# Layer 1 of a four-layer graph network: the W1v g products of two blocks as four 64x64 products on the quarters of TensorE

## The chip, the cores and the metric

The kernel runs on one core of one Trainium2 chip. The metric is the device time of one execution in microseconds (us). TensorE, VectorE, ScalarE and GpSimd are called PE, DVE, ACT and POOL in the profile; PEld is the loading of weights into TensorE, which overlaps its products.

## What is computed

Four graph layers, each a residual with a layer norm ahead of it, work on x of shape (8, 2048, 64) with one normalised adjacency matrix adj of 2048 x 2048. The change is in layer 1, which takes three steps:

```python
def _L1_gnn_ref(causal_vars, adj_matrix, intervention_value, W1, b1, W2, b2, intervention_idx):
    v = causal_vars.at[:, intervention_idx].set(intervention_value)
    for _ in range(MAX_STEPS):                                   # 3
        effects = jnp.einsum('nm,bmd->bnd', adj_matrix, v)
        h = jnp.concatenate([v, effects], axis=-1)
        h = jax.nn.relu(jnp.einsum('bnk,dk->bnd', h, W1) + b1)   # W1 is 64 x 128
        v = jnp.einsum('bnk,dk->bnd', h, W2) + b2
    return v
...
h = jnp.maximum(_layernorm(x, axis=-1), 0.0)
x = x + _L1_gnn_ref(h, adj, ...)
```

W1 falls into a half for v (W1v) and a half for the neighbours' sum (W1e). So each step needs W1v v, and adj times W1e v.

## The kernel before

**Two batches share the 128 partitions.** A tile in feature layout is 128 x 512: partitions 0 to 63 hold the 64 features of one batch, 64 to 127 those of the next, and the 512 columns are nodes. The 8 batches are NP = 4 pairs p, and the 2048 nodes are NB = 4 blocks nb. The weights are laid out to match, as 128 x 128 matrices with the 64 x 64 weight twice on the diagonal and zeros elsewhere (`make_weights`, L620 to L633). All of layer 1 stays in the form g, the value after the relu: from the second step on W2 is multiplied into the weights, so that W1v v is `w1v2` times g (in the first step `w1vT` times v), with the biases folded in.

**One block of one step** (`layer1`, L869 to L925) is made of these parts:

- `product` (L243 to L254): adj times the node-layout tiles u for the block's 512 nodes. For each of 16 chunks m it issues two matmuls (H and L, the high and low parts of u in a reduced fp32 format, L250, output `bv`), 32 in all. Its argument `fill` names work that is put into TensorE's program behind chunk m. Then `scaled` (L240, on VectorE) multiplies by the row `crow` into the tile g.
- `ph` (L897, L900 to L902): W1v times the block's old g, called gT here. It is an fp32 product of the full array, 128 x 128 weights and 512 columns, put behind m = 12, into a PSUM bank of the tag "tr".
- L904, on VectorE: g = ph + g. L905, on ScalarE: g = relu(g + bias).
- `finish` (L876 to L886) turns a finished g back to nodes with four small products (`back_to_nodes`, L661 to L666, in PSUM tiles of the tag "big"), and in the first two steps splits the result into H and L for the next step (`halves`, L230 on ScalarE and L232 on VectorE). It stands behind the product of the next block, so that the relu has time; that of the third block is put behind m = 8 of the fourth.

Around these, VectorE tests in the first two steps that the adjacency has the expected form (L846), and the last step prepares the next pair p (`prepare_next`, L672 to L684: transposes into gT by `to_feat`, L267 the copy) and the norm ahead of layer 2.

**PSUM** has eight banks: the tags "mm" (product), "tr" (transposes, ph) and "big" (two banks to a tile), two buffers each. **The order** of each engine's work is the program's, except where a planner moves an instruction behind others because it reckons that its operands come later, and where `tc.issue_after` ties one instruction behind another.

**Layer 0 has the only products of this kernel that divide the array.** `node_weights` (L697 to L728) works on 64 of the 128 partitions at a time (`bb` = 0 and 1, output `y`, L711), each with 64 x 128 weights and 512 columns, into a PSUM bank of its own. They are used below as a yardstick.

Of the kernel before, what the change touches and what calls it, by code (L numbers as in the profile page):

```python
# [8 lines left out]
F32 = mybir.dt.float32  # L9
# [5 lines left out]
ALU = mybir.AluOpType  # L15
# [27 lines left out]
def uniform_path(  # L43
# [30 lines left out]
    nc = tc.nc  # L74
    P = 128
    B, N, C = x.shape
# [9 lines left out]
    psums = [pro.enter_context(tc.tile_pool(name="psump", bufs=1, space=bass.MemoryType.PSUM))]  # L86
# [14 lines left out]
    def bank(tag, name):  # L101
        return psums[-1].tile([P, 512], F32, tag=tag, name=name)
# [31 lines left out]
    def nodes(acc):  # L134

        return acc.rearrange("p j f -> p (j f)").rearrange("p (e j c) -> p j e c", e=2, c=C)

    def load_x(layer, p, nb, queue=nc.sync):
        acc = block("acc", f"acc_{layer}_{p}_{nb}", 2)
        fill_x(acc, layer, p, nb, queue)  # L140
        return acc
# [11 lines left out]
    def load_crow(nb, name, tag="crow"):  # L153
        t = work.tile([P, 512], F32, tag=tag, name=f"crow_{name}", bufs=2)
        nc.sync.dma_start(t, crowD[:, nb * 512:(nb + 1) * 512].to_broadcast([P, 512]))
        return t
# [4 lines left out]
    def split(t):  # L161
        return t.rearrange("p j (b c) -> p j b c", b=2)
# [45 lines left out]
    def go_on():  # L208

        with tc.issue_after(ahead.pop().ins) if ahead else nullcontext():  # L210
            for e in list(pending):
                next(e[0])
                e[1] -= 1
                if e[1] == 0:
                    pending.remove(e)
        ahead.clear()
# [8 lines left out]
    def halves(src, name, pool=None, later=None):  # L225

        pool, bufs = (work, 6) if pool is None else (pool, 4)
        Hq = pool.tile([P, 4, 2 * C], F32R, tag="H", name=f"H_{name}", bufs=bufs)
        Lq = pool.tile([P, 4, 2 * C], F32R, tag="L", name=f"L_{name}", bufs=bufs)
        copies.append(nc.scalar.copy(Hq, src))  # L230
        def rest():
            lows.append(nc.vector.tensor_tensor(Lq, src, Hq.bitcast(F32), op=ALU.subtract))  # L232

        rest() if later is None else later.append(rest)
        return Hq, Lq
# [9 lines left out]
    def product(hl, nb, name, out, crow, fill={}, tag="mm"):  # L245

        ps = bank(tag, f"bv_{name}")
        for m in range(NCH):
            for i in range(2):
                nc.tensor.matmul(  # L250
                    ps, hl[m // 4][i][:, m % 4, :], BT[:, m, nb * 512:(nb + 1) * 512],
                    start=(m == 0 and i == 0), stop=(m == NCH - 1 and i == 1),
                )
            if m in fill:  # L254
                fill[m]()
        return scaled(ps, out, crow)
# [308 lines left out]
    nm = "0_1_3a"  # L565
    tx = work.tile([P, 512], F32, tag="z", name=f"t1T_{nm}", bufs=3)
    ps = bank("b1", f"bv_{nm}")
    for m in range(NCH):
        if m in (2, 7, 12):
            go_back(1 + m // 5)  # L570
        for i in range(2):
            nc.tensor.matmul(
                ps, hls[1][m // 4][i][:, m % 4, :], BT[:, m, 3 * 512:],
                start=(m == 0 and i == 0), stop=(m == NCH - 1 and i == 1),
# [80 lines left out]
    def feat(i, name):  # L655

        if i == 0:
            return term(1, name)
        return lastp[0].tile([P, 512], F32, tag="fm", name=name, bufs=4)

    def back_to_nodes(fT, wmat, name, tag="big"):  # L661

        ps = psums[-1].tile([P, 4, 2 * C], F32, tag=tag, name=f"bn_{name}")
        for t in range(4):
            nc.tensor.matmul(ps[:, t, :], fT[:, t * P:(t + 1) * P], wmat, start=True, stop=True)  # L665
        return ps  # L666
# [5 lines left out]
    def prepare_next(n, q):  # L672
        if n >= len(items):
            return
        layer, p = items[n]
        nm = f"{layer}_{p}_{q}"
        hl, gT = ops.setdefault(n, ([], []))
        h = load_h(p, q, nm, lastp[0] if n else l0q)
        if layer == 1:
            if q == 0:  # L680
                nc.scalar.copy(h[0:1, 0, :], ivt)
            gT.append(to_feat(h, feat(0, f"gT_{nm}"), nm))
            h = back_to_nodes(gT[q], w1e, f"u_{nm}", "big" if n else "mm")
        hl.append(halves(h, nm))  # L684

    def rows4(r):
        return r.rearrange("p (b c) -> p b c", b=2)[:, None].to_broadcast([P, 4, 2, C])

    def keep(p, nb, acc, name, more):

        norm_relu(acc, name, lambda z: nc.gpsimd.dma_start(hs[p][:, part(nb), :], z))  # L691
        nc.gpsimd.tensor_tensor(nodes(acc), nodes(acc), more, op=ALU.add)  # L692
        kept.append(nc.gpsimd.dma_start(xs[p][:, part(nb), :], acc))
# [36 lines left out]
    def feat_0(p, q):  # L730
        h = load_h(p, q, f"f0_{p}_{q}", l0q)
        return to_feat(h, term(0, f"t0T_{p}_{q}"), f"0_{p}_{q}")

    first_t0 = []
    for p in range(NP):
# [47 lines left out]
        for nb in range(NB):  # L783
            nm = f"0_{p}_{nb}b"
# [3 lines left out]
                fill={12: lambda: first_t0.append(feat_0(0, 0))} if p + nb == 0 else {},  # L788
                tag="mm" if p + nb else "b0",
# [32 lines left out]
    w1vT, w1eT, w2T, wos, w1v2, w1e2, r1e, rbo = (wl[:, i, :] for i in range(8))  # L822
# [18 lines left out]
    def test(k):  # L841

        i, q = divmod(k, NB)
        st, mt = tested[k]
        junk = lastp[0].tile([P, 512], U8, name="junk")
        nc.vector.scalar_tensor_tensor(  # L846
            junk, mt, cols[:, i, :], st, op0=ALU.mult, op1=ALU.not_equal,
            accum_out=bad[:, i, q:q + 1],
        )
        test_load()  # L850
# [18 lines left out]
    def layer1(n, p):  # L869
        hl, gT = ops[n]  # L870
        steps = 3
        for s in range(steps):
            last = s == steps - 1
            g_new, hl_new = [], []

            def finish(nb):  # L876
                nm = f"1_{p}_{s}_{nb}"
                if last:
                    acc = load_x(1, p, nb)
                    pn = back_to_nodes(g_new[nb], w2T, nm)  # L880
                    nc.vector.tensor_tensor(nodes(acc), split(pn), nodes(acc), op=ALU.add)
                    keep(p, nb, acc, f"2_{p}_{nb}", rows4(rbo))
                else:
                    pn = back_to_nodes(g_new[nb], w1e2, nm)
                    nc.vector.tensor_tensor(split(pn), split(pn), rows4(r1e), op=ALU.add)
                    hl_new.append(halves(pn, nm))  # L886

            def mid():
                if last:
                    prepare_next(n + 1, 2)  # L890
                else:
                    finish(2)

            for nb in range(NB):
                nm = f"1_{p}_{s}_{nb}"
                crow = load_crow(nb, nm)
                ph = bank("tr", f"ph_{nm}")  # L897
                g = feat((s + 1) % 2, f"g_{nm}")
                fill = {8: mid} if nb == 3 else {}
                fill[12] = lambda: nc.tensor.matmul(  # L900
                    ph, w1v2 if s else w1vT, gT[nb], start=True, stop=True
                )  # L902
                product(hl, nb, nm, g, crow, fill=fill)
                gadd = nc.vector.tensor_tensor(g, ph, g, op=ALU.add)  # L904
                nc.scalar.activation(g, g, AF.Relu, bias=b1s if s else b1c)  # L905
                g_new.append(g)
                go_on()
                if nb in (1, 2):
                    finish(nb - 1)
                    if last:  # L910
                        prepare_next(n + 1, nb - 1)
                if s < 2:
                    k = 2 * (8 * p + 4 * s + nb)
                    with tc.issue_after(gadd.ins):
                        test(k)
                        test(k + 1)
            if last:
                finish(2)
                prepare_next(n + 1, 3)
            if last and n == NP - 1:  # L920

                put_off.append(lambda: finish(3))
            else:
                finish(3)
            gT, hl = g_new, hl_new  # L925
# [81 lines left out]
    for n, (layer, p) in enumerate(items):  # L1007
        (layer1, layer2)[layer - 1](n, p)
        if n == NP - 1:
            test_end()  # L1010
# [593 lines left out]
```

## Time and profile before

The median of three runs is 1248.38 us (1244.74 to 1248.88). The profiled run has a span of 1245.5 us.

| | |
|---|---|
| TensorE busy | 1211.7 us of the span |
| VectorE / ScalarE / GpSimd busy | 745.5 / 181.7 / 223.9 us |
| layer 1, about | 632 to 1085 us |
| the largest two groups of bv (L250), H and L | 426.3 and 401.0 us busy, 1024 matmuls each |
| ph (L900) | 48 products, 96 matmuls |
| granted TensorE clock | 0.994 |

In the page's groups a product in full fp32 shows up as two matmuls with the same names, and two weight loads. A matmul's end is modelled and its start is recorded, so what a matmul takes of TensorE is read from the distance of starts. The chain that ended last is followed back from the last instruction of the kernel, each time to what released it; the share of an engine in it is the share of the span in which that engine's work, and not a wait for another, held up the end.

### The profile page before, as it was taken

What the parts mean: (1) busy time and instruction counts of PE and PEld (TensorE: products, weight loads), DVE (VectorE), ACT (ScalarE), POOL (GpSimd) and SP (SyncE); (2) the same over time, 40 slices, a digit from 0 to 9 for tenths busy, and PEclk for the clock granted to TensorE, in tenths of its full rate; (3) what the DMA queues carried; (4) which work ended last, traced back from release to release, by engine and by line L of the source; (5) the groups of instructions that cost most, each with busy time, mean ns of one, the idle gap of its engine ahead of it and who ended that gap; (6) DMA issues with size and microseconds to landing.
All of it is one profiled execution on the core that took longest, in us unless ns stands there. A gap on an engine that the chain in (4) does not pass through costs nothing.

```text
span 1245.5 us, 15336 instructions
## 1 busy us (share of the span) xinstructions
PE 1211.7 (97%) x5702; PEld 860.6 (69%) x5702; DVE 745.5 (60%) x1940; ACT 181.7 (15%) x281; POOL 223.9 (18%) x233
## 2 busy tenths in 40 slices
PE   5999999999999999999999999999999999999995
PEld 4775555555665557655577888788788878888884
DVE  5356888777757774477654445445543545566664
ACT  6610001000010000000111121112111211211100
POOL 5410222211131111011110022003101300231211
PEclk9999999999999999999999999999999999999998
DMA  9951334332332232122265436533643553433311
GB/s 358 372 142 53 101 107 115 85 87 72 90 106 67 65 89 79 51 64 64 60 148 135 110 100 153 116 90 119 161 106 90 152 127 96 128 137 117 115 56 46
DMA packets 100984, 140.98 MB, mean 113 GB/s; under 512 B 43772, under 2 KB 58108, under 8 KB 98852
## 3 DMA queue, kind: packets, MB, share of 16 engines
q1 hardware_dynamic: 82820, 80.74, 24.8%
q0 software_dynamic: 11776, 48.15, 13.0%
q10 hardware_dynamic: 6304, 11.01, 2.7%
q8 instruction: 47, 0.77, 0.2%
q14 instruction: 37, 0.30, 0.1%
HBM read 95.03 MB, written 35.66 MB: 105 GB/s over the span
## 4 chain that ended last, share of the span: by engine, by line
PE 93%; DMA 3%; DVE 3%; POOL 1%; issue 0%; ACT 0%; SPq 0%; POOLq 0%; ACTq 0%
PE bv L250 38%; PE y L711 26%; PE bn L665 5%; PE ph L900 3%; PE bv_2b L250 2%; PE bv_1b L250 2%; PE bv_3b L250 2%; PE bv_0b L250 2%; DMA BT<-in_adj_dram 2%; PE bn_u L665 1%; PE bv_0a L250 1%; PE bv_3a L250 1%; PE pt L262 1%; PE bv_2a L250 1%; PE pS L949 1%; PE bv_1a L250 1%
## 5 line engine op out<-in xcount | busy, mean ns | idle before, releaser
L250 PE MATMUL bv<-BT,H 128*128 128x512 f32 x1024 | 426.3, 416 | 0.0
L250 PE MATMUL bv<-BT,L 128*128 128x512 f32 x1024 | 401.0, 392 | 0.0
L250 PEld LDWEIGHTS bv<-BT,H 128*128 128x128 f32 x1024 | 192.5, 188 | 47.8 <-issue 11.6
L250 PEld LDWEIGHTS bv<-BT,L 128*128 128x128 f32 x1024 | 192.7, 188 | 47.5 <-issue 11.5
L720 DVE SCALAR_TENSOR_TENSOR acc<-y,emb,acc 128x128 f32<-128x128 f32 x512 | 176.2, 344 | 65.7 <-PE y L711 65.7
L720 DVE SCALAR_TENSOR_TENSOR odd<-y,emb,odd 128x128 f32<-128x128 f32 x448 | 153.3, 342 | 0.0
L711 PE MATMUL y<-wt,t0T 64*128 64x512 f32 x512 | 143.7, 607 | 2.4 <-DVE odd L720 1.7
L240 DVE TENSOR_TENSOR g<-bv,crow 128x512 f32<-128x512 f32 x48 | 33.2, 692 | 183.2 <-PE bv L250 183.2
L194 POOL TENSOR_TENSOR rstd<-var,mhalf 128x8 f32<-128x8 f32 x64 | 105.7, 1653 | 180.6 <-DVE var L191 174.8
L186 ACT ACTIVATE sq<-z 128x512 f32<-128x512 f32 x64 | 40.4, 631 | 406.6 <-DVE z L181 396.6
L711 PEld LDWEIGHTS y<-wt,t0T 64*128 64x128 f32 x512 | 45.8, 185 | 63.3 <-issue 57.1
L692 POOL TENSOR_TENSOR acc<-acc,b2r 128x512 f32<-128x512 f32 x16 | 22.2, 1389 | 315.5 <-DVE z L181 315.5
L692 POOL TENSOR_TENSOR acc<-acc,wl 128x512 f32<-128x512 f32 x16 | 20.7, 1291 | 299.3 <-DVE z L181 299.2
L711 PE MATMUL y<-wt,t1T 64*128 64x512 f32 x256 | 66.8, 589 | 0.0
L197 DVE SCALAR_TENSOR_TENSOR z<-z,rstd 128x512 f32<-128x512 f32 x64 | 44.7, 703 | 35.5 <-POOL rstd L194 35.5
L665 PEld LDWEIGHTS bn<-wl,g 128*128 128x128 f32 x384 | 49.5, 191 | 5.1 <-ACT g L905 1.5
L189 DVE TENSOR_REDUCE var<-sq 128x8 f32<-128x512 f32 x64 | 43.6, 681 | 15.6 <-ACT sq L186 15.6
L665 PE MATMUL bn<-wl,g 128*128 128x128 f32 x384 | 51.1, 276 | 0.0
L846 DVE SCALAR_TENSOR_TENSOR junk<-mt,cols,st 128x512 uint8<-128x512 bf16 x64 | 47.7, 745 | 4.1 <-DMA mt<-MD 3.7
L711 PEld LDWEIGHTS y<-wt,t1T 64*128 64x128 f32 x256 | 27.1, 187 | 27.8 <-issue 27.8
L905 ACT ACTIVATE g<-g,b1s 128x512 f32<-128x512 f32 x32 | 23.2, 724 | 137.2 <-DVE g L904 137.1
L691 POOL DMA_DIRECT2D hs<-z x32 | 18.6, 582 | 133.6 <-DVE z L197 97.0
(210 smaller groups left out, 1672.4 us busy)
## 6 DMA issues: line engine op xcount, KB each, us to landing
BT<-in_adj_dram POOLq DMA_DIRECT2D x16, 1024.0 KB, 19.5
crow<-crowD SPq DMA_DIRECT2D x64, 256.0 KB, 3.3
st<-in_adj_dram SPq DMA_DIRECT2D x64, 256.0 KB, 3.6
hs<-z POOLq DMA_DIRECT2D x40, 256.0 KB, 3.2
xs<-acc POOLq DMA_DIRECT2D x32, 256.0 KB, 2.4
MD<-BT POOLq DMA_DIRECT2D x16, 512.0 KB, 5.6
acc<-xs SPq DMA_DIRECT2D x32, 256.0 KB, 3.9
hb<-hs SPq DMA_DIRECT2D x28, 256.0 KB, 3.3
```

The costliest lines, as they stand in the source:

```text
L186: squares.append(nc.scalar.activation(sq, z, AF.Square))
L189: nc.vector.tensor_reduce(var, groups(sq), axis=AX.X, op=ALU.add)
L194: powers.append(nc.gpsimd.tensor_tensor(rstd, var, mhalf, op=ALU.pow))
L197: scales.append(nc.vector.scalar_tensor_tensor(groups(h), g, 0.0, rstd[:, :, None].to_broadcast([P, 8, C]), op0=ALU.max, op1=ALU.mult))
L240: ahead.append(nc.vector.tensor_tensor(to, ps.rearrange("p (q t) -> p t q", t=4), crow, op=ALU.mult))
L250: nc.tensor.matmul(ps, hl[m // 4][i][:, m % 4, :], BT[:, m, nb * 512:(nb + 1) * 512], start=(m == 0 and i == 0), stop=(m == NCH - 1 and i ...
L665: nc.tensor.matmul(ps[:, t, :], fT[:, t * P:(t + 1) * P], wmat, start=True, stop=True)
L692: nc.gpsimd.tensor_tensor(nodes(acc), nodes(acc), more, op=ALU.add)
L711: nc.tensor.matmul(y[:, bb, :], terms[k][hs_, ts], wt[hs_, k, dg * 512:(dg + 1) * 512], start=(k == 0), stop=(k == K - 1),)
L720: last = nc.vector.scalar_tensor_tensor(xj, yd, ec, old, op0=ALU.mult, op1=ALU.add)
L846: nc.vector.scalar_tensor_tensor(junk, mt, cols[:, i, :], st, op0=ALU.mult, op1=ALU.not_equal, accum_out=bad[:, i, q:q + 1],)
L900: fill[12] = lambda: nc.tensor.matmul(ph, w1v2 if s else w1vT, gT[nb], start=True, stop=True)
```

## The change

The product of the full array multiplies two 64 x 64 blocks of zeros along with the two that count. The change takes two blocks nb and nb + 1 together and gives each quarter of the array one product of its own: the two batches (bb) of two blocks (i). Weights of batch bb are on its partitions, and the output of the second block comes out on the partitions of the other batch (`two[bb ^ i]`), so that the four products lie on four different quarters. They write two PSUM banks, one for each half of the rows, in a tile of the tag "big". ScalarE then copies each quarter to where its old g was (gT, in place), on the partitions of its batch, and L904 adds that tile instead of the PSUM bank. The four products stand behind m = 10 of the even blocks; the odd blocks have none. The aim is that the four products take the time of one.

```diff
+            def map_two(nb):
+
+                ph = psums[-1].tile([P, 2, 512], F32, tag="big", name=f"ph_1_{p}_{s}_{nb}")
+                w = w1v2 if s else w1vT
+                two = (slice(0, C), slice(C, P))
+                for i in range(2):
+                    for bb in range(2):
+                        nc.tensor.matmul(
+                            ph[two[bb ^ i], bb, :], w[two[bb], two[bb]], gT[nb + i][two[bb], :],
+                            start=True, stop=True,
+                        )
+                for i in range(2):
+                    for bb in range(2):
+                        nc.scalar.copy(gT[nb + i][two[bb], :], ph[two[bb ^ i], bb, :])
+
             for nb in range(NB):
                 nm = f"1_{p}_{s}_{nb}"
                 crow = load_crow(nb, nm)
-                ph = bank("tr", f"ph_{nm}")
                 g = feat((s + 1) % 2, f"g_{nm}")
                 fill = {8: mid} if nb == 3 else {}
-                fill[12] = lambda: nc.tensor.matmul(
-                    ph, w1v2 if s else w1vT, gT[nb], start=True, stop=True
-                )
+                if nb % 2 == 0:
+                    fill[10] = lambda: map_two(nb)
                 product(hl, nb, nm, g, crow, fill=fill)
-                gadd = nc.vector.tensor_tensor(g, ph, g, op=ALU.add)
+                gadd = nc.vector.tensor_tensor(g, g, gT[nb], op=ALU.add)
                 nc.scalar.activation(g, g, AF.Relu, bias=b1s if s else b1c)
```

## The prediction

> **What bounds the kernel now.** I read the page from the top (busy shares, then the chain of work that ended last), then the groups and busy times of the stretch in which layer 1 runs, then single instructions around one of the products that the change touches.
>
> ```profile
> PE 1211.7 (97%) x5702; PEld 860.6 (69%) x5702; DVE 745.5 (60%) x1940; ACT 181.7 (15%) x281; POOL 223.9 (18%) x233
> PE 93%; DMA 3%; DVE 3%; POOL 1%; issue 0%; ACT 0%; SPq 0%; POOLq 0%; ACTq 0%
> PE bv L250 38%; PE y L711 26%; PE bn L665 5%; PE ph L900 3%; PE bv_2b L250 2%; PE bv_1b L250 2%; PE bv_3b L250 2%; PE bv_0b L250 2%; DMA BT<-in_adj_dram 2%; PE bn_u L665 1%; PE bv_0a L250 1%; PE bv_3a L250 1%; PE pt L262 1%; PE bv_2a L250 1%; PE pS L949 1%; PE bv_1a L250 1%
> ```
>
> TensorE is 93% of the chain, and the products that change (ph, L900) are 3% of it. The table by stretches says how tight layer 1 is (columns: length, then busy time and instructions of PE, weight loads, VectorE, ScalarE, GpSimd):
>
> ```profile
> 632.00:1085.00 453.00, 453.00 (x2159) 363.73 (x2159) 217.13 (x418) 78.54 (x128) 59.48 (x59) 1.00 0.50 122
> L904 DVE TENSOR_TENSOR g<-ph,g 128x512 f32<-128x512 f32 x48 | 33.0, 688 | 1.1
> L267 ACT COPY gT<-pt 128x512 f32<-128x512 f32 x12 | 7.0, 586 | 60.1 <-PE pt L262 60.1
> PEld bn L665 <- ACT g L905: 1.5, 8, 0.2
> ```
>
> TensorE has no gap in 453 us, at full clock; VectorE is busy 48% of it and ScalarE 17%. TensorE waits for a relu (L905) for 1.5 us in all. So in this stretch a microsecond of TensorE taken away or added is a microsecond of the span, and the other engines have room.
>
> What one ph costs is read from starts, since ends are modelled (columns: start, length, engine):
>
> ```profile
> 689.90 0.39 PE L250 MATMUL bv<-BT,L 128*128 128x512 f32 x1
> 690.13 1.02 PE L900 MATMUL ph<-g,wl 128*128 128x512 f32 x2
> 690.58 0.80 PE L250 MATMUL bv<-BT,H 128*128 128x512 f32 x1
> 691.22 0.40 PE L250 MATMUL bv<-BT,L 128*128 128x512 f32 x1
> ```
>
> From one bv to the bv after next, without a ph, it is 2 x 0.227 = 0.454 us (starts 689.90 and 690.13 are 0.23 apart). Here it is 691.22 - 689.90 = 1.32. So one ph, an fp32 product written as two matmuls of 0.43 us each, costs 0.867 us; taken over all 48 of them the median is 0.868. In all 48 x 0.868 = 41.7 us, the 3% of the chain.
>
> The trace has no 64x64 quarter. It has the nearest thing, the y products of layer 0 (L711): 64 rows x 128 columns, bb = 0 on the upper and bb = 1 on the lower half of the rows, each two matmuls again:
>
> ```profile
> 401.14 1.05 PE L711 MATMUL y<-wt,t1T_1a 64*128 64x512 f32 x4
> 402.00 1.05 PE L711 MATMUL y<-wt,t2T_1b 64*128 64x512 f32 x4
> 401.14 0.22 PEld L711 LDWEIGHTS y<-wt,t1T_1a 64*128 64x128 f32 x2 [0.21 <-issue]
> ```
>
> Four matmuls, which are two whole products, take 0.86 us: the two halves of the rows run side by side. More than that: the four fill 1.05 = 0.43 + 0.59 + 0.03, so they start in two pairs, 0.03 apart within a pair (two loads of 0.187 fill 0.22). Had the second product waited for the second matmul of the first, as program order has it, four would fill three steps, 1.45. So a product on other rows overtakes the second half of the one before it.
>
> Those groups also show what it costs to change the division of the array:
>
> ```profile
> 412.44 1.05 PE L711 MATMUL y<-wt,t2T_1b 64*128 64x512 f32 x4
> 413.42 0.50 PE L250 MATMUL bv_2b<-BT,H_t 128*128 128x512 f32 x1
> 413.75 0.39 PE L250 MATMUL bv_2b<-BT,L_t 128*128 128x512 f32 x1
> ...
> 420.81 0.60 PE L262 MATMUL pt<-ident,hb_f 128*128 128x128 f32 x4
> 421.34 1.13 PE L711 MATMUL y<-wt,t0T 64*128 64x512 f32 x4
> 422.30 1.02 PE L711 MATMUL y<-wt,t1T_2a 64*128 64x512 f32 x4
> ```
>
> Out: the y group would be done at 412.44 + 0.86 = 413.30, and the second bv would start at 413.53; it starts at 413.75, 0.22 late (0.21 to 0.24 over 15 such places). In: the four transposes end their turn at 420.81 + 4 x 0.107 = 421.24; the second k would start at 422.10 and does at 422.30, 0.20 late (0.20 in nearly all). A round trip costs 0.43 us.
>
> **What the Trainium skill says.** "TensorEngine Tiling (Array Packing)", Key Properties: tiles work independently, and a change of tiling mode drains TensorE. The trace agrees for row tiles, with 0.43 us for a round trip. "TensorE: Matmul & The Clock Gate", Part 3, has single-pass products on tiles divided both ways running together, 16 of them 10.6 times as fast; it also says that matmuls start in strict program order. The first half isn't shown here for column tiles; the second disagrees with the y group above, and the trace decides. "FP8 and Floating Point Precision", TensorE Precision Notes: true fp32 takes four passes; the two matmuls of 0.43 us per ph fit that. "PSUM — Partial Sum Buffer", on bank collisions: different row tiles must not write one bank together. The change gives each half of the rows its own bank, so nothing has to be serialised for that.
>
> **The change part by part.** Per pair of blocks (24 pairs: 4 p x 3 s x 2):
> - *Removed:* two ph, 2 x 0.868 = 1.736 us of TensorE, on the path.
> - *Added on TensorE:* one round trip, 0.435 by the y groups (bounds 0.3 to 0.7, as the columns are divided too), and four products as eight matmuls. If all four quarters run together, as the two row halves do, that is 2 x 0.43 + about 0.06 of starts one after another (the pairs above were 0.03 apart) = 0.92. If only the rows overlap, it is twice that of a y pair: 1.72. If a row half takes its matmuls strictly in order but lets the two column halves overlap, there are three steps: 1.29. I take 0.92: the overtaking seen in y says that a matmul waits for its own tile and not for the stream, and the four tiles share neither rows with columns nor banks across rows.
> - *Sum for the likeliest case:* 1.736 - 0.92 - 0.435 = 0.38 us per pair, x 24 = 9.1 us.
> - *ScalarE:* four copies of 64x512, priced at the 0.586 us of the 128x512 copy from PSUM (fewer partitions, same elements in each): 2.34 us per pair, 56 us over layer 1, so ScalarE goes from 17% to 30% busy. Nothing of it is on the path: the map stands after m = 10, so 10 bv (2.27 us) of the product follow. The copies for the even block are done some 1.2 to 1.4 us after the map, 1 us before the block's bv end; L904 comes 0.9 us after the end (bv end 692.38, L904 at 693.30). The other two copies end about 0.2 us after it, still before L904, and the block they are for comes a product (9 us) later. Behind the copies on ScalarE stand the relu L905, 1.6 us after the product's end, and the H copies of a block finished at the start of the product, done long before.
> - *VectorE:* L904 reads two SBUF tiles in place of PSUM and SBUF; a sum of two SBUF tiles (L727) takes 679 ns, L904 688. It now waits for ScalarE instead of TensorE; behind it is the test L846, with no hurry. Cost nothing.
> - *PSUM:* two banks of the tag "big" for about 3.5 us per pair, next to the back_to_nodes tiles (L663). There are two buffers, and those tiles come every few microseconds; the next one after a map takes the other buffer. In the last step, where two come together, the second needs the map's: it follows transposes and a copy, by then the map is copied. Nothing, at most 0.5 us in 4 places.
> - *Order:* nothing is waited for earlier than before, except that gT of the second block is read one product sooner; it is a step old.
>
> **The rivals.**
> - *Three steps* (a row half is in order): 24 x (1.736 - 1.29 - 0.435) = 0.3 us less, 1248. For it: the overtaking is shown between rows only. Against: I know of no reason why columns should differ.
> - *Columns don't overlap*: 24 x (1.72 + 0.435 - 1.736) = 10 us more, 1258.4, slower. For it: both column halves of a row half are fed from the same 64 partitions, and no column tile is in the trace. Against: the skill's 16 tiles.
> - *The copies become a wait*: were relu, and with it a back_to_nodes, 0.5 us late in the 8 places that have no slack (the 1.5 us row) the gain would shrink by 4 us, to 1243.
>
> **How the numbers follow.** Before: 1248.38, with 1244.74 lowest. Quarters together: 0.57, 1248.4 - 9.1 = 1239.3. Three steps: 0.20, 1248. Columns in turn: 0.18, 1258. Late copies: 0.05, 1243. The range runs from 1235.5 (a cheap round trip of 0.3, 12.4 us saved) to 1251 (three steps with a dearer round trip), which leaves out columns in turn and a little at the ends. Faster by over 3.7 us: the first case less a tenth for a dear round trip, and half of the fourth, 0.55. Within: 0.23. Slower: 0.22.
>
> **What would show it.** Right: from the last bv before the map to the second bv after it about 0.45 + 1.35 us; eight ph matmuls in two clumps 0.43 apart; layer 1 some 9 us shorter with TensorE still without a gap; ScalarE near 135 us in it. Three clumps and 0.45 + 1.73 is the first rival, four clumps the second. Idle time of bn L665 before ScalarE's g beyond 1.5 us would be the third. The prediction is wrong if entering or leaving quarters costs far more than 0.43 us, or a column half has to wait for the other.

## The result and the profile after

The changed kernel takes 1239.24 us (median of 4, 1238.1 to 1241.54) where the kernel before takes 1247.76 (median of 4, 1244.74 to 1248.88): a ratio of 0.9938, with a 95% interval of 0.9915 to 0.9961. Run once more beside the experiments it gave 1237.89 us and 0.9923 (0.9908 to 0.9937). So it is 8 to 10 us faster, and the 1239.3 of the prediction was met. How it was met is another matter: two terms were off, in opposite directions, and they nearly cancel.

The page after, first the busy time by engine, then the chain that ended last:

```profile
PE 1197.7 (97%) x5798; PEld 843.7 (68%) x5798; DVE 744.7 (60%) x1940; ACT 237.0 (19%) x377; POOL 223.5 (18%) x233
PE 92%; DMA 3%; DVE 3%; issue 1%; POOL 1%; ACT 0%; SPq 0%; POOLq 0%; ACTq 0%
```

TensorE is 14.0 us less busy, ScalarE 55.3 us busier, the others as before. But 14 us is more than the gain, and the chain has a new 1%: "issue", time in which TensorE waited for nothing that the profile names.

The first visit to the quarters in TensorE's timeline (start, length), and the weight loads at its head:

```profile
634.02 0.39 PE L250 MATMUL bv<-BT,L 128*128 128x512 f32 x1
634.34 1.09 PE L901 MATMUL ph<-gT,wl 64*64 64x512 f32 x8
635.36 0.50 PE L250 MATMUL bv<-BT,H 128*128 128x512 f32 x1
635.69 0.39 PE L250 MATMUL bv<-BT,L 128*128 128x512 f32 x1
...
634.34 0.21 PEld L901 LDWEIGHTS ph<-gT,wl 64*64 64x64 f32 x8 [0.35 <-issue]
```

From bv to the second bv after is 635.69 - 634.02 = 1.67, less 2 x 0.227: 1.22 us for four products, and it is 1.22 in all 24 visits. The eight matmuls start in two clumps: four within 0.02 us, and four more 0.48 us later (eight of 0.59 fill 1.09 = 0.50 + 0.59). So all four first halves start ahead of all second halves: no quarter waits for another.

The stretch of layer 1, the ScalarE copies, and TensorE's waits in it:

```profile
632.00:1085.00 453.00, 450.41 (x2296) 356.79 (x2295) 220.34 (x426) 134.63 (x225) 65.64 (x65) 1.00 0.51 128
L907 ACT COPY g<-ph 64x512 f32<-64x512 f32 x64 | 37.2, 581 | 49.6 <-PE ph L901 48.8
PEld bn L665 <- issue: 3.0, 1, 3.0
PEld bn_u L665 <- ACT gT L267: 2.8, 12, 0.2
PEld bn L665 <- ACT g L918: 1.6, 8, 0.2
```

The copies take 581 ns, ScalarE comes to 135 us, and bn waits for ScalarE's g as little as before (1.6 us). What is new is a single wait of 3.0 us, and TensorE's 453 us have a hole of 2.6. It is early in layer 1. The timeline of TensorE there, then ScalarE's:

```profile
644.80 0.39 PE L250 MATMUL bv<-BT,L 128*128 128x512 f32 x1
647.77 1.74 PE L665 MATMUL bn<-wl,g 128*128 128x128 f32 x8 [2.59 <-issue]
649.16 0.77 PE L250 MATMUL bv<-BT,H 128*128 128x512 f32 x1
649.73 0.63 PE L250 MATMUL bv<-BT,L 128*128 128x512 f32 x1
650.16 0.63 PE L250 MATMUL bv<-BT,H 128*128 128x512 f32 x1
...
646.75 0.30 ACT L681 COPY hb<-ivt 1x128 f32<-1x128 f32 x1 [8.83 <-DMA acc<-xs]
646.96 1.33 ACT L918 ACTIVATE g<-g,b1c 128x512 f32<-128x512 f32 x2
```

The first bn of layer 1 needs the relu of the first block (L918). That relu's operand was ready at about 639.8 (L917, on VectorE, ran at 639.17 for 0.68), yet it ran at 646.96, behind L681: a copy of 128 numbers into hb, a tile of the *next* pair, ahead of which ScalarE stood idle for 8.8 us, waiting for a load. (The profile names the load of acc; the load of hb itself was issued 0.7 us before that one. In the kernel before it names the load of hb.) There the same two instructions stand the other way round:

```profile
641.03 0.72 ACT L905 ACTIVATE g<-g,b1c 128x512 f32<-128x512 f32 x1 [5.88 <-DVE var L191]
647.87 0.30 ACT L681 COPY hb<-ivt 1x128 f32<-1x128 f32 x1 [6.12 <-DMA hb<-hs]
```

And after the hole TensorE was slow: bv starts are 0.43 apart instead of 0.227, bn starts 0.21 instead of 0.11. The table by stretches (the seventh column of numbers, ahead of the DMA share and GB/s, is the granted clock):

```profile
644.00:648.00 4.00, 1.41 (x8) 0.90 (x7) 1.89 (x3) 1.25 (x3) 0.60 (x1) 1.00 0.87 290
648.00:652.00 4.00, 4.00 (x16) 3.42 (x16) 2.45 (x5) 0.87 (x2) 0.00 (x0) 0.57 1.18 267
```

Where the time went can be summed by steps. Layer 1 is 12 steps (4 pairs x 3); from the first bv of one step to that of the next, the last one to the first bv of layer 2. The three steps shown are those of the first pair:

| us | step 1 | step 2 | step 3 | all 12 |
|---|---|---|---|---|
| before | 35.46 | 36.30 | 40.94 | 452.1 |
| after | 38.83 | 35.22 | 39.96 | 443.9 |

Every step but the first is 1.0 to 1.1 us shorter, which is 12 to 13 us over the layer; the first is 3.4 us longer, so it gave back some 4.4. The net is 8.2 us. (The profiled spans differ by 9.4; 1.5 us of that lies before layer 1, and 0.3 us goes the other way after it, where the change is not.)

### The profile page after: what moved, and what is told of

It reads as the page before. It is cut to its first block, busy times and chain, and to the rows that moved or that the text cites. A ratio compares the mean times of both kernels' runs of the same rounds, so it can differ in the third digit from the quotient of the medians.

```text
span 1236.1 us, 15662 instructions
## 1 busy us (share of the span) xinstructions
PE 1197.7 (97%) x5798; PEld 843.7 (68%) x5798; DVE 744.7 (60%) x1940; ACT 237.0 (19%) x377; POOL 223.5 (18%) x233
## 4 chain that ended last, share of the span: by engine, by line
PE 92%; DMA 3%; DVE 3%; issue 1%; POOL 1%; ACT 0%; SPq 0%; POOLq 0%; ACTq 0%
PE bv L250 38%; PE y L711 26%; PE bn L665 5%; PE bv_1b L250 2%; PE bv_3b L250 2%; PE bv_2b L250 2%; PE bv_0b L250 2%; PE ph L901 2%; DMA BT<-in_adj_dram 2%; PE bn_u L665 1%; PE bv_0a L250 1%; PE bv_3a L250 1%; PE pt L262 1%; PE bv_2a L250 1%; PE pS L962 1%; PE bv_1a L250 1%
## 5 line engine op out<-in xcount | busy, mean ns | idle before, releaser
L250 PE MATMUL bv<-BT,H 128*128 128x512 f32 x1024 | 409.7, 400 | 0.0
L907 ACT COPY g<-ph 64x512 f32<-64x512 f32 x64 | 37.2, 581 | 49.6 <-PE ph L901 48.8
L181 DVE TENSOR_TENSOR z<-acc,mean 128x512 f32<-128x512 f32 x56 | 38.3, 692 | 6.0 <-DMA hs<-z 4.6
```

The costliest lines, as they stand in the source:

```text
L181: firsts.append(nc.vector.tensor_tensor(split(z), nodes(xt), each(mean)[:, :, :, None].to_broadcast([P, 4, 2, C]), op=ALU.subtract))
L250: nc.tensor.matmul(ps, hl[m // 4][i][:, m % 4, :], BT[:, m, nb * 512:(nb + 1) * 512], start=(m == 0 and i == 0), stop=(m == NCH - 1 and i ...
L907: nc.scalar.copy(gT[nb + i][two[bb], :], ph[two[bb ^ i], bb, :])
```

## The experiments

The theory after the result: the quarters save 1.736 - 1.218 = 0.52 us per pair of blocks, 12.4 us in all; a visit costs 0.36 us for changing the division plus 0.86 us for each four products; and 4.4 us are lost to the order on ScalarE. The rivals are named with each run. The first four runs were timed beside one set of runs of the kernel before (1247.67 us), the last three beside another (1246.69 us). Between executions the first bv of layer 1 starts up to 4 us earlier or later (628.3 to 632.0 us in these traces), so a small difference is read from the steps of layer 1 rather than from the whole time.

**The changed kernel again** (`a0_after`, no edit), to see whether the wait is an accident.

> The changed kernel once more, on the chip and beside the runs of the others. Theory (twelve steps of layer 1 save 1.04 us each on TensorE, 12.4 us, and the first step gives 4.4 us back at one wait): about 1239, 8 to 9 us under the kernel before, and the wait of about 3 us of the first bn of layer 1 is in the trace again. Rival (that wait was an accident of one run): about 1235, no such wait.

It gave 1237.89 us, 9.8 us under the kernel before and so a little faster than expected, and the wait was there again, 2.8 us. The first step took 38.64 us, the others what they took above. The wait was not an accident; the rival falls.

**The small copy behind the relu** (`e1_relu_first`). In `prepare_next`, where `relus` collects the results of L918:

```diff
-                nc.scalar.copy(h[0:1, 0, :], ivt)
+                with tc.issue_after(relus[-2].ins) if relus else nullcontext():
+                    nc.scalar.copy(h[0:1, 0, :], ivt)
```

> The changed kernel with one edit: the small ScalarE copy of iv into the next pair's h (L681) is tied behind the relu of the last step, so that it can't stand ahead of the first relu of layer 1. Theory (that copy, waiting for its load, held up the relu, the relu the first bn, and the pause halved TensorE's speed for a while after): the wait and the slow stretch go, 4.4 us less than the changed kernel, 1234 to 1236, and the first step of layer 1 saves 1.04 us like the others. Rival (the first bn waits for something else, the copies of the quarters or the test loads): the wait stays, 1239.

1233.62 us, ratio 0.9893 (0.9878 to 0.9909), 4.3 us less than the changed kernel beside it. ScalarE's timeline at the start of layer 1, and TensorE's stretch:

```profile
635.46 2.37 ACT L909 COPY gT<-ph 64x512 f32<-64x512 f32 x4 [1.86 <-PE ph L903]
639.85 0.72 ACT L920 ACTIVATE g<-g,b1c 128x512 f32<-128x512 f32 x1 [2.02 <-issue]
...
632.00:1085.00 453.00, 453.00 (x2320) 359.44 (x2319) 224.36 (x433) 135.05 (x226) 66.22 (x66) 1.00 0.52 129
```

The relu runs at 639.85 with no L681 ahead of it, TensorE has no hole, and the first step takes 34.39 us, 1.07 less than before the change, like the others. The twelve steps take 439.4 us, 12.7 less than before: the 12.4 of the quarters, and 0.3 over. What held up TensorE was not the four copies themselves, which are still there, but a copy that belongs to the next pair.

**One visit per step in place of two** (`e3_once`; the tie of the last run is kept in this and all that follow):

```diff
-                if nb % 2 == 0:
-                    fill[10] = lambda: map_two(nb)
+                if nb == 0:
+                    fill[10] = lambda: [map_two(0), map_two(2)]
```

> As e1_relu_first, but both maps of a step, all eight quarter products, stand behind m = 10 of the first block: one visit to the quarters per step in place of two. Theory (a visit costs 0.36 us for the change of division and each four quarters 0.86 us): 12 visits fewer, 4.3 us less than e1_relu_first, about 1230.5; from the bv before to the second bv after 0.45 + 2.08 us. Rival (the 0.36 us belongs to each four products, as loads of weights and starts one after another, not to the visit): the same as e1_relu_first, 1235.

1228.71 us, ratio 0.9854 (0.9839 to 0.9869), 4.9 us less than with two visits (4.3 were expected).

```profile
633.15 0.39 PE L250 MATMUL bv<-BT,L 128*128 128x512 f32 x1
633.47 1.95 PE L903 MATMUL ph<-gT,wl 64*64 64x512 f32 x16
635.34 0.50 PE L250 MATMUL bv<-BT,H 128*128 128x512 f32 x1
635.68 0.40 PE L250 MATMUL bv<-BT,L 128*128 128x512 f32 x1
```

635.68 - 633.15 - 0.45 = 2.08 = 2 x 0.86 + 0.36. The 0.36 belongs to the visit, so 12 fewer of them are 4.3 us; the rival would have shown 2.44. The steps got shorter by 5.4 in the trace. Of the 1.1 us more, some 0.7 lie in the bv right after a visit, which stand a little wide (in sum 0.040 us after each of the 24 visits, 0.022 after each of the 12); why they do was not looked into. This is the fastest kernel of the study, ahead of both the kernel before and the changed one.

**Two quarters in place of four** (`e4_same`): both blocks on the diagonal, the second block's outputs in the other bank.

```diff
-                            ph[two[bb ^ i], bb, :], w[two[bb], two[bb]], gT[nb + i][two[bb], :],
+                            ph[two[bb], bb ^ i, :], w[two[bb], two[bb]], gT[nb + i][two[bb], :],
...
-                        nc.scalar.copy(gT[nb + i][two[bb], :], ph[two[bb ^ i], bb, :])
+                        nc.scalar.copy(gT[nb + i][two[bb], :], ph[two[bb], bb ^ i, :])
```

> As e1_relu_first, but the second block's outputs come out on the same partitions as the first's, in the other bank, so that both blocks use the same two quarters of the array, the ones on the diagonal, and the other two stay idle. Theory (the gain is that four different quarters run side by side): four clumps of starts in place of two, 0.86 us more per pair of blocks, 24 x 0.86 = 20.6 us more than e1_relu_first, about 1256, slower than the kernel before. Rival (the smaller weights or the row halves alone make it cheap): within 2 us of e1_relu_first.

1255.66 us, ratio 1.0061 (1.0044 to 1.0078): slower than the kernel before, and 22.0 us more than with four quarters (19.8 in the steps of the traces; 20.6 were expected).

```profile
636.81 0.39 PE L250 MATMUL bv<-BT,L 128*128 128x512 f32 x1
637.13 1.93 PE L903 MATMUL ph<-gT,wl 64*64 64x512 f32 x8
638.99 0.50 PE L250 MATMUL bv<-BT,H 128*128 128x512 f32 x1
639.33 0.40 PE L250 MATMUL bv<-BT,L 128*128 128x512 f32 x1
```

2.07 us per visit, in four clumps of two. This is what the prediction's second rival, columns that take turns, would have looked like (it put it at 1258.4). The same eight matmuls of 64x64 on two quarters cost 0.85 us more than on four: the gain comes from the second pair of quarters, and not from the smaller weights or the row halves.

**Full-array products in the new frame** (`e2_full`): grouping, tag, ScalarE copies and the sum from SBUF stay.

```diff
...
+                for i in range(2):
+                    nc.tensor.matmul(ph[:, i, :], w, gT[nb + i], start=True, stop=True)
...
+                        nc.scalar.copy(gT[nb + i][half, :], ph[half, i, :])
```

> As e1_relu_first, but the two blocks' products are full-array ones again (128x128 weights, two of them behind m = 10 of the even blocks, into the two banks of the big tile); grouping, PSUM tag, the ScalarE copies and the sum of two SBUF tiles stay as changed. Theory (only the four quarters save time, the rest of the change is off the path): the time of the kernel before, 1246 to 1249. Rival (part of the gain comes from the grouping, the PSUM tag or VectorE's operands): some of the 14 us stays, below 1243.

1245.51 us, ratio 0.9993 (0.9987 to 1.0000), half a microsecond under the range expected, in a set of runs in which the kernel before was a microsecond lower too. In the trace two products cost 1.72 us, no more than two ph before (1.736), so nothing is paid for a change of division. Everything in the change but the quarters is worth about 0.9 us, at most some 1.6 (the interval's end); the steps of layer 1 are 0.6 us shorter than before the change.

**Every copy twice** (`e5_twice`), the second with the same values:

```diff
+                        for _ in range(2):
-                        nc.scalar.copy(gT[nb + i][two[bb], :], ph[two[bb ^ i], bb, :])
+                            nc.scalar.copy(gT[nb + i][two[bb], :], ph[two[bb ^ i], bb, :])
```

> As e1_relu_first, with each of the 96 ScalarE copies made twice, the second writing the same values again. Theory (the copies are beside the path with room to spare): ScalarE 56 us busier, the time within 1 us of e1_relu_first, 1233 to 1235. Rival (the copies are near the limit of their room): relu and the following bn late, several us more, and idle time of bn before ScalarE's g well over 1.6 us.

1235.13 us, ratio 0.9907 (0.9890 to 0.9924). By times it can't be told from the run with single copies (0.9878 to 0.9909), but the middle is 1.7 us higher, where at most 1 was expected. The steps of layer 1 are 1.1 us longer, and the trace shows where:

```profile
L910 ACT COPY g<-ph 64x512 f32<-64x512 f32 x128 | 74.4, 581 | 50.5 <-PE ph L903 47.9
PEld bn_u L665 <- ACT g L910: 2.2, 3, 0.7
PEld bn L665 <- ACT g L921: 1.6, 8, 0.2
```

With 56 us more on ScalarE the relu is not late anywhere (1.6 us as ever). The first to suffer are three bn_u, 0.7 us each, in the last steps of the first three pairs, where two tiles of the tag "big" are wanted close together; these steps take 40.33 to 40.36 us instead of 39.96. Single copies hold nothing up; double ones are at the limit in one place.

**Row halves with all columns** (`e6_rows`): four products of 64 rows and 128 columns, four banks.

```diff
...
-                            ph[two[bb ^ i], bb, :], w[two[bb], two[bb]], gT[nb + i][two[bb], :],
+                            ph[i][:, bb, :], w[two[bb], :], gT[nb + i][two[bb], :],
...
-                        nc.scalar.copy(gT[nb + i][two[bb], :], ph[two[bb ^ i], bb, :])
+                        nc.scalar.copy(gT[nb + i][two[bb], :], ph[i][two[bb], bb, :])
```

> As e1_relu_first, but the four products of a map use 64 rows and all 128 columns (the weights' other columns are zero), each into a bank of its own, so that the array is divided by rows alone, as for y. Two run side by side, so two rounds of 0.86 us. Theory (what made the way into the quarters cheaper than the way into y, 0.14 against 0.20 us, is the narrower weights, loaded in 0.130 instead of 0.187 us with nothing over them): from the bv before to the second bv after 0.45 + 2.13 us, with 0.20 of it on the way in. Rival (row halves are dearer to enter in the y groups for what stands before them there, transposes and waits): 0.45 + 2.08, with 0.14 on the way in. About 1257 in either case.

1256.01 us in one run.

```profile
636.01 0.39 PE L250 MATMUL bv<-BT,L 128*128 128x512 f32 x1
636.33 1.99 PE L906 MATMUL ph<-gT,wl 64*128 64x512 f32 x8
638.25 0.50 PE L250 MATMUL bv<-BT,H 128*128 128x512 f32 x1
638.59 0.40 PE L250 MATMUL bv<-BT,L 128*128 128x512 f32 x1
```

638.59 - 636.01 - 0.45 = 2.13 (2.12 from the unrounded starts), against 2.07 on two quarters. The first clump starts 0.32 us after the bv in both; the second starts 0.533 us after the first instead of 0.480, and the weight loads take 0.187 us instead of 0.133. So row halves cost 0.05 us more on the way in though bv stands before them here too, and the rival falls. The kernel before has one y group right behind a bv that says the same:

```profile
598.45 0.39 PE L250 MATMUL bv_3b<-BT,L_t 128*128 128x512 f32 x1
598.77 1.13 PE L711 MATMUL y<-wt,t0T 64*128 64x512 f32 x4
599.73 1.02 PE L711 MATMUL y<-wt,t1T_3a 64*128 64x512 f32 x4
```

Its first start is 0.32 us after the bv, 0.09 late, and the next group follows after 0.96 us where 0.86 is usual: again 0.19 to 0.20 on the way in. That the longer loads are the cause fits the size (0.054 us each), but it isn't shown: the run changes the width of the weights and the division of the columns together.

## Why the prediction came out right

- **TensorE is the bound, microsecond for microsecond: right**, once the hole is gone. Without it, the steps lost 12.7 us and the time about 13 (ratio 0.9893 of 1247.67 is 13.3).
- **The four quarters run together, 0.92 us: right**, a little better. They take 0.86 + 0.02: starts within a clump are 0.007 apart, not 0.03. The reading of the y group, that a matmul waits for its own tile and not for the stream, carried over from rows to columns. It takes for granted that the two halves of a product stand together in TensorE's program; the profile records their starts, and not how the program holds them. Both TensorE rivals fall: three steps would be 1.29 us and three clumps, and columns in turn is what the run on two quarters shows.
- **The round trip, 0.435 us: mis-sized.** With the clump's width it is 0.36 in all, not 0.06 + 0.435 = 0.495. The way out cost 0.22, as read from y; the way in 0.14 instead of 0.20: the second clump starts 0.48 us after the first and not 0.53 as in y, as with the wider weights of `e6_rows`. The 0.22 is counted from the first start of a group, so the spread of the starts (0.035 us in y, 0.020 here) is already in it; the prediction added 0.06 for that spread once more. It bounded the round trip by 0.3 to 0.7 and took the y groups' value whole, without asking what it was made of. This makes the saving 0.52 us per pair and 12.4 in all, where 0.38 and 9.1 were forecast.
- **Copies off the path, 581 ns each: right**, and the PSUM tiles too: bn_u's wait went from 2.5 to 2.8 us. The third rival, late copies, fell; twice the copies didn't bring it about. But the loss that it named, 4 us by a late relu, did come, in one place and by another cause. The row that the prediction would have watched for it, bn before ScalarE's g, stayed at 1.6 us: the profile books the new wait of 3.0 us under "issue".
- **"Behind the copies on ScalarE stand the relu L905, ... and the H copies": this step failed.** It listed the queue by the program of layer 1 alone. On ScalarE the planner had put L681, which belongs to the next pair, between them, ahead of the first relu. In the kernel before it stood just behind that relu, where the profile showed it waiting 6.1 us at no cost. In the changed kernel the order is turned, and a wait that had been free came onto the path: 2.6 us of hole and 1.7 of slow clock, 4.3 measured by taking it away. Which part of the change made the planner turn the two round, the four copies or something else, and by what reckoning, was not looked into.
- **The sum:** 9.1 forecast; 12.4 less 4.3 to 4.4 is 8 found. That the time came out on the forecast is luck, two errors against each other. The mechanism, four products in the time of one on an engine that bounds the layer, was right by itself.

## What to carry to other kernels

Here two products side by side in row halves were good evidence for four in quarters, and the price of changing the division was paid per visit: gather all products that use a division into one visit, as the run with one visit a step did for 4.9 us more. Before pricing added work on an in-order engine at nothing, list what else stands in that engine's queue at that place, also from other parts of the program, and what it waits for: an instruction with a long, free wait, one place behind the one that matters, is a risk when an edit can make a planner reorder them. When a change hits its number, still sum its steps; here the sum showed 4.3 us left to take.

## What was not expected of the hardware

- A pause of TensorE costs more than its length. After the 2.6 us hole the granted clock was 0.57 over the stretch from 648 to 652 us, and bn and bv ran at about half speed for some 3.4 us: 1.7 us on top of 2.6. The Trainium skill, "TensorE: Matmul & The Clock Gate", HAM oscillation, has the clock halve after idle gaps of more than about 3.4 us. Here a distance of 2.98 us between two starts was enough, and of 2.79 us in the second run of the changed kernel. Nor is there a fixed limit in these traces: in the first run a distance of 2.81 us, from 48.50 to 51.31, left the clock at 1.00 from 48 to 56 us.
- Quarters are entered more cheaply than row halves (0.14 against 0.20 us), by about as much as their weight loads are shorter (0.133 against 0.187 us).
- Four first halves start within 0.02 us, and the four second halves 0.48 us later, though the kernel calls the products one after another. If the two halves of a product stand together in TensorE's program, matmuls overtake across columns as well as across rows.
